# A Mamba block and an FFN on one core: how many gate blocks the first phase leaves to the scan

## The chip, the cores and the metric

The kernel runs on one core of a Trainium2 chip. The core has TensorE (PE in the profile), VectorE (DVE), ScalarE (ACT), GpSimd (POOL) and SyncE (SP), which here issues every DMA. The metric is the device time in microseconds, as the median over several executions. Before the change it is 4656.46 us, from three executions between 4654.45 and 4663.09 us.

## The reference, cut to what matters

Two layers with residuals and layer norms, for 2 sequences of 4096 tokens of width 512:

```
h_in, gate = split(x_norm @ in_proj_w.T)           # 1024 channels each
u  = silu(conv4(h_in) + conv_b)
ts, Bm, Cm = split(u @ x_proj_w.T)                  # 128, 16, 16
dt = softplus(ts @ dt_proj_w.T + dt_proj_b)
h[t] = exp(dt * A) * h[t-1] + dt * u * Bm           # 16 states a channel
y  = (sum_n h * Cm + D * u) * silu(gate)
x  = x + norm(y @ out_proj_w.T)
x  = x + norm(ffn(norm(x)))                         # 512 -> 2048 -> 512, relu,
                                                    # 4-bit weights with LoRA terms
```

What matters here is `silu(gate)`: it is needed only at the end of the scan, so the product `x_norm @ in_proj_w.T` for its 1024 channels can be made at any time before the scan comes to those tokens.

## The kernel before

Tokens are cut into 16 groups of 512 (`NG`, `G`), and a group into four blocks of 128 tokens (`J`). Every product of full precision is three matmuls (`mm3`, L98): both operands are split into a high and a low part in fp32r.

**Phase A** (to L703) goes through the groups, and in each through 8 channel blocks (`block(g, ib)`, L510). A block makes h_in of 128 channels (`h_mm`, 12 matmuls of 512 columns), its convolution (`h_conv`, three DVE instructions), u and its split (`h_rest`), the x_proj sums of an earlier block (`x_proj`), and for the group before it dt (`dt_mm`, softplus) and its transposes (`q_out`). In `ib == 7` the next group's x is transposed into `xnh` and `xnl` (`turn_x`, L163: four PE transposes, an ACT copy, a DVE subtraction); nothing of the next group can start without them. Between all this, FFN weights are dequantised (`prep_ffn`) and stored.

The gate is made in *gate blocks* (`gate_block`, L446): 128 tokens by 512 channels, 12 matmuls of 512 columns, a silu on ACT, a store to `g_d`. A group has 8 of them (four rows of tokens, two halves of channels). Groups 0, 1 and 15 make all 8 in phase A. Groups 2 to 14 make the blocks of rows 0 and 1 there, one each at `ib` 0, 3, 4 and 7 (the tuple on L547), and leave rows 2 and 3 to the scan: for these `turn_x` stores the split x to `xg_d` (L171). 13 groups times 2 rows are 26 blocks for each half of the channels.

**Phase B** (from L706) is the scan. Its unit of order is the *slot*: one DVE scan instruction (`scan`, L950) of 8 states by 64 tokens by 128 channels; there are 2080. For a slot PE makes the input term b (`make_b`, two matmuls of 256 columns), ACT makes exp(dt*A) (`make_exp`, L921), POOL multiplies h by C (L977), and PE sums over states with transposes into PSUM (`nsum`, L997). `slots[e]` is the slot at which group e's last scan is done.

Beside the scan runs a list of other PE work, `tail(g)`, one per stage. A stage begins at slot `start[g]`, ten slots before a group's scans are done: `start` is 0, 134, 262, 390 and so on, 128 or 144 slots apart. Stage 0 holds the gate blocks that were left, first half of the channels (`gates(0)`, L1023). Stage 1 holds the out_proj of the first group (`out_proj`, L1121), then the second half (`gates(1)`). Stages 2 to 15 hold the out_proj of a group and the FFN of the one before.

The pace is a budget in `pe[0]` (L1485): each matmul adds its assumed cost, and after each slot work is taken from the tail until the budget for that slot is used. `GD` (L1083) is a cost without work: a pause before the first gate block of a half. What is left of a tail when its stage ends is emitted at once (L1473). ACT, SP, PE and POOL keep the order in which this program emits, except around the seam between A and B, where the two phases' instructions are interleaved; DVE is ordered by a scheduler.

In `gates`, x of a block is fetched two blocks ahead (`x_in`), its PSUM result is copied to SBUF (L1063), and four results together (`GB`, L1084) get their silu (L1070), so that ACT changes between the tables of exp and silu once per four blocks; then they are stored to `g_d`. SP issues all of it in one queue, with the scan's loads.

Of the kernel before, what the change touches and what calls it, by code (L numbers as in the profile page):

```python
# [8 lines left out]
F32 = mybir.dt.float32  # L9
# [5 lines left out]
P = 128  # L15
# [5 lines left out]
def f32(ap):  # L21
    return ap.bitcast(F32)
# [3 lines left out]
def kernel(  # L26
# [7 lines left out]
    nc = tc.nc  # L34
# [7 lines left out]
    KH, KI, KF = H // P, I // P, HID // P  # L42
# [3 lines left out]
    dram = ctx.enter_context(tc.tile_pool(name="dram", bufs=1, space=DRAM))  # L46
# [9 lines left out]
    NG, J = NT // G, G // P  # L56
# [5 lines left out]
    g_d = [dram.tile([KI, G, P], F32, name=f"g_d{g}") for g in range(NG)]  # L62
    B_d = dram.tile([2, NT, 2, N], F32, name="B_d")
    C_d = dram.tile([NB, NW, N, U], F32, name="C_d")
    GS, JS = 2, 2
    xg_d = [dram.tile([J - JS, P, 2, KH, P], F32, name=f"xg_d{g}") for g in range(NG - 1)]
    wg_d = [dram.tile([P, KH, 512], F32, name=f"wg_d{k}") for k in range(4)]
    y_d = [dram.tile([KI, G, P], F32, name=f"y_d{g}") for g in range(NG)]
    x1_d = [dram.tile([J, P, H], F32, name=f"x1_d{g}") for g in range(NG)]
# [47 lines left out]
    with ExitStack() as sa:  # L117
# [15 lines left out]
        ps_m = sa.enter_context(tc.tile_pool(name="psA", bufs=2, space=PSUM))  # L133
        ps_t = sa.enter_context(tc.tile_pool(name="ptA", bufs=2, space=PSUM))
# [28 lines left out]
        def turn_x(g, xt, j, pool=ps_t):  # L163

            tp = pool.tile([P, KH, P], F32, name=f"tp{g}_{j}", tag="m" if pool is ps_m else "t")
            for kt in range(KH):
                nc.tensor.transpose(tp[:, kt, :], xt[j][:, kt * P:(kt + 1) * P], ident)
            s = slice(j * P, (j + 1) * P)
            nc.scalar.copy(xnh[:, :, s], tp)
            nc.vector.tensor_sub(xnl[:, :, s], tp, f32(xnh[:, :, s]))  # L170
            if j >= JS and GS <= g < NG - 1:  # L171
                for e, t in enumerate((xnh, xnl)):
                    nc.sync.dma_start(xg_d[g][j - JS, :, e], f32(t[:, :, s]))

        def prep_split(w, store, nm, l):

# [319 lines left out]
        GATES = {0: [(j, hf) for hf in range(2) for j in range(J)], 1: [(j, hf) for j in range(J) for hf in range(2)]}  # L496
        GPL = {0: (0, 0, 0, 2, 2, 2, 1, 1), 1: (1,) * 8, NG - 1: (1, 1, 1, 1, 1, 1, 0, 0)}
# [3 lines left out]
        def gate(g, st, fs):  # L501

            if st["gates"]:
                fs.append(gate_block(g, st, *st["gates"].pop(0)))
# [5 lines left out]
        def block(g, ib):  # L510
# [12 lines left out]
            fs = []  # L523

            def evict():
                while fs:
                    fs.pop(0)()
# [9 lines left out]
            def q():  # L537
                if qm:
                    q_out(*qm.pop(0))
# [4 lines left out]

            def gates(late=False):
                if st and late == (2 <= g < NG - 1):
                    for _ in range(GPL.get(g, (1, 0, 0, 1, 1, 0, 0, 1))[ib]):  # L547
                        gate(g, st, fs)


# [1 line left out]
            if ib == 0:  # L552
                q()
            elif ib in (1, 2):
                z(2)
            elif ib == 7 and g + 1 < NG:
                left = {j for j, _ in st["gates"]} if g >= 2 else {J - 1}
                if g < 2:
                    gates()
                    evict()  # L560
                turn = [j for j in range(J) if j not in left] + sorted(left)
                for pool in (ps_m, ps_t):
                    turn_x(g + 1, st["xt"], turn.pop(0), pool)
            if b and ib != 4:
                h_rest((b - 1) // KI, last, (b - 1) % KI)
# [77 lines left out]
            if old:  # L643
                for _ in range(MPL[ib]):
                    i = old["muls"]
# [11 lines left out]

        for g in range(NG):
            groups[g] = {"pm": {}, "u": [], "us": [], "v": [], "muls": 0,
                         "gates": list(GATES.get(g, GATES[1][:2 * JS] if g < NG - 1 else GATES[1]))}  # L660
            if g == 0:
                halo_in(0, 0)
            for ib in range(KI):
                block(g, ib)
            groups.pop(g - 1, None)

        g, old, fs = NG, groups[NG - 1], []
# [6 lines left out]
        x_proj(NG - 1, old, KI - 1)  # L674
        x_out(NG - 1, old)
        gate(NG - 1, old, fs)
        while qm:
            q_out(*qm.pop(0))
        for f in fs:
            f()  # L680
        while dq:
            dq.pop(0)()
        dus.append((NG - 1, old, KI - 1))
# [22 lines left out]
    with ExitStack() as sb:  # L706
# [80 lines left out]
        now, due = [0], {}  # L787

        def at(t, f):
            due.setdefault(max(t, now[0] + 1), []).append(f)  # L790
# [138 lines left out]
        pe = [0.0]  # L929
        TB, TT, TM = 0.125, 0.107, 0.235  # L930
# [92 lines left out]
        def gates(hf, following):  # L1023

            w = [c1.tile([P, KH, 512], FR, name=f"wg{hf}_{e}", tag="xh" if e == 0 else "xl") for e in range(2)]
            for kt in range(KH):
                for e in range(2):
                    nc.sync.dma_start(f32(w[e][:, kt]), wg_d[2 * hf + e][:, kt])
            if hf:
                yield  # L1030

            def x_in(g, j):
                t = wn_.tile([P, 2, KH, P], FR, name=f"xg{hf}_{g}_{j}", tag="wn")
                nc.sync.dma_start(f32(t), xg_d[g][j - JS])
                return t

            todo_ = [(g, j) for g in range(GS, NG - 1) for j in range(JS, J)]
            held = []

            def let_go(f):  # L1040

                while f in held:
                    held.pop(0)()

            raw, nxt = [], [x_in(*q) for q in todo_[:1 + hf]]
            pe[0] += GD[hf]
            yield
            for i, (g, j) in enumerate(todo_):
                t = nxt.pop(0)
                if i == 0 and not hf:  # L1050
                    nxt.append(x_in(*todo_[1]))
                if i >= len(todo_) - 2:
                    following.send(None)
                if len(held) > 1:
                    let_go(held[0])
                pm = (ps_a if hf else ps_w).tile([P, 512], F32, name=f"pz{hf}_{g}_{j}", tag=f"a{i % J}" if hf else "w")
                for kt in range(KH):
                    mm3b(pm, t[:, 0, kt], t[:, 1, kt], w[0][:, kt], w[1][:, kt], kt == 0, kt == KH - 1)
                    yield
                    if kt == 1 and i + 2 < len(todo_):  # L1060
                        nxt.append(x_in(*todo_[i + 2]))
                z = row(f"z{hf}_{g}_{j}")
                held.append(lambda z=z, pm=pm: nc.scalar.copy(z, pm))  # L1063
                at(now[0] + 2, lambda f=held[-1]: let_go(f))
                raw.append((g, j, z))
                if len(raw) == GB or i == len(todo_) - 1:
                    def silu(raw=raw):
                        let_go(held[-1] if held else None)
                        for _, _, z in raw:
                            nc.scalar.activation(z, z, AF.Silu)  # L1070

                    def store(raw=raw):
                        for g_, j_, z in raw:
                            nc.sync.dma_start(g_d[g_][4 * hf:4 * hf + 4, j_ * P:(j_ + 1) * P, :].rearrange("k p i -> p k i"), z.rearrange("p (k i) -> p k i", i=P))

                    at(now[0] + 3, silu)
                    at(now[0] + 5, store)
                    raw = []
            let_go(held[-1] if held else None)
            ahead[hf] = following.send(None)  # L1080
            yield

        GD = 6.5, 10.0  # L1083
        GB = 4  # L1084

        def new_acc(nm):
            return [ps_a.tile([P, H], F32, name=f"{nm}_{j}", tag=f"a{j}") for j in range(J)]
# [323 lines left out]
        C1 = KI * J * (3 * TM + TT)  # L1411
        CF = KF * (KH + J) * 3 * TM + J * KH * TT
# [13 lines left out]
        LEAD = 0  # L1426
        PH = 10
        start = [LEAD] + [slots[e] - PH for e in ends]

        def tick():  # L1430

# [33 lines left out]
        todo, g = iter(()), -1  # L1465
        for k in range(len(units)):
            exp = make_exp(k + 1) if k + 1 < len(units) else iter(())
            n = slots[k + 1] - slots[k]
            for i in range(n):
                slot = slots[k] + i  # L1470
                assert slot == now[0]
                if g < NG and slot >= start[g + 1]:
                    for _ in todo:  # L1473
                        pass
                    g += 1
                    todo, pe[0] = tail(g), 0.0
                    cost = C1 + CF if g > 1 else (C1 if g else 0) + KH * 3 * TM * (NG - 1 - GS) * (J - JS) + GD[g]
                    length = start[g + 1] - start[g] if g < NG else 2 * U
                    cost += length * (2 * TB + (2 * NH + 1) * TT / NU)
                for _ in range(3 if n > 2 else 1):  # L1480
                    next(exp, None)
                scan(k, i // 2, i % 2, slot)
                make_b(slot + 2)
                tick()
                while g >= 0 and pe[0] < cost * (slot + 1 - start[g]) / length and next(todo, 0) is None:  # L1485
                    pass
            for _ in exp:
                pass
# [57 lines left out]
```

## Time and profile before

| | us |
|---|---|
| median of three executions | 4656.46 |
| the profiled execution | 4660.94 |
| its span | 4659.1 |
| phase A, to the first scan | 995.0 |
| first ten slots (scans) | 50.4 |
| rest of stage 0, 124 slots | 180.4 |
| stage 1, 128 slots | 220.3 |
| stage 2, 128 slots | 211.5 |
| stage 3, 128 slots | 210.1 |

The profile comes from one execution. *Busy* is the time in which an engine's instructions ran; matmuls are pipelined and their ends are modelled (a 512-column matmul is shown with 0.39 us where the next starts 0.23 us later), so a gap that PE shows is idle for certain, and small waits are hidden. *PEclk* is the TensorE clock granted, 1.00 being full speed. The DMA share is the mean busy share of the 16 DMA engines and can go a little over 1 in a short window.

### The profile page before, as it was taken

How to read it: one execution, taken by the hardware profiler on the slowest of the kernel's cores; microseconds unless marked ns; L12 is line 12 of the kernel's file. 1: busy time of each engine (PE TensorE's matmuls, PEld its weight loads, DVE VectorE, ACT ScalarE, POOL GpSimd, SP SyncE). 2: the span in 40 equal slices, each digit the busy share in tenths (PEclk: the TensorE clock that was granted, in tenths of full speed). 3: DMA queues.
4: the chain of work that ended last, by engine and by line, in shares of the span. 5: the costliest groups of instructions: out<-in, count | busy, mean ns of one | idle time of the engine just before them, and what ended most of it. 6: DMA issues, size and time to landing. Idle time of an engine off the chain costs nothing.

```text
span 4659.1 us, 85017 instructions
## 1 busy us (share of the span) xinstructions
PE 4485.4 (96%) x26613; PEld 3872.2 (83%) x26613; DVE 3845.0 (83%) x6273; ACT 3308.1 (71%) x7324; POOL 3274.7 (70%) x2360
## 2 busy tenths in 40 slices
PE   8999999968899999999999989999999999999999
PEld 6777777757788888888888878888888888888887
DVE  6677777749888999999999989899999999999931
ACT  5777777768688676767677767777686767767643
POOL 1333333339797888889898889888898988888820
PEclk9999999979999999999999999999999999999999
DMA  4888888768889888879788877788797878888765
GB/s 146 260 253 256 258 257 257 231 188 227 244 223 258 228 240 222 251 219 261 220 247 226 239 200 227 229 231 253 211 261 219 253 215 247 226 240 237 218 233 195
DMA packets 1139315, 1083.93 MB, mean 233 GB/s; under 512 B 142583, under 2 KB 912399, under 8 KB 1138872
## 3 DMA queue, kind: packets, MB, share of 16 engines
q1 hardware_dynamic: 1138872, 1078.50, 80.2%
q8 instruction: 220, 3.60, 0.3%
q14 instruction: 223, 1.83, 0.1%
HBM read 800.87 MB, written 277.29 MB: 231 GB/s over the span
## 4 chain that ended last, share of the span: by engine, by line
PE 73%; DMA 7%; DVE 6%; POOL 5%; ACT 4%; issue 3%; SPq 2%; DVEq 0%; POOLq 0%; ACTq 0%
PE yp L997 15%; PE b L947 8%; PE pu L99 5%; PE pu L100 5%; PE pu L101 5%; PE fa L99 4%; PE fa L100 4%; PE fa L101 4%; DVE h L965 3%; POOL pr L977 3%; PE pm L100 2%; PE pm L99 2%; PE pm L101 2%; POOL bd L807 2%; PE pg L99 1%
## 5 line engine op out<-in xcount | busy, mean ns | idle before, releaser
L977 POOL TENSOR_TENSOR pr<-h,cb 128x1008 f32<-128x1008 f32 (+1 forms) x1056 | 2453.3, 2336 | 474.2 <-DVE b L964 276.7
L965 DVE TENSOR_TENSOR_SCAN h<-dA,b 128x512 f32<-128x512 f32 x2080 | 2535.4, 1220 | 142.0 <-PE b L947 13.7
L921 ACT ACTIVATE dA<-dt,A 128x252 f32<-128x252 f32 x4096 | 1702.4, 496 | 161.1 <-DVE h L965 145.5
L997 PE MATMUL yp<-ident,pr 128*126 128x128 f32 (+1 forms) x8448 | 1104.7, 274 | 19.1 <-DVE xl L1260 7.4
L997 PEld LDWEIGHTS yp<-ident,pr 128*126 128x126 f32 (+1 forms) x8448 | 951.4, 140 | 28.3 <-POOL pr L977 10.5
L947 PEld LDWEIGHTS b<-bd,d 128*128 128x128 f32 x4160 | 752.1, 189 | 215.3 <-POOL bd L807 21.6
L947 PE MATMUL b<-bd,d 128*128 128x256 f32 x4160 | 875.2, 291 | 54.5 <-DMA d<-dT_d 17.9
L1307 ACT ACTIVATE pu<-pu,bu 128x512 f32<-128x512 f32 x256 | 168.7, 659 | 602.5 <-PE pu L101 602.5
L437 DVE SCALAR_TENSOR_TENSOR pm<-hin,cw,pm 128x512 f32<-128x512 f32 x384 | 288.0, 750 | 210.9 <-ACT pm L434 203.8
L99 PE MATMUL fa<-wn,hh 128*128 128x512 f32 x1024 | 421.2, 411 | 0.0
L99 PE MATMUL pu<-xh,wu 128*128 128x512 f32 x960 | 402.3, 419 | 7.6 <-DMA wu<-wu_d 7.4
L100 PE MATMUL fa<-wn,hh 128*128 128x512 f32 x1024 | 403.6, 394 | 0.0
L101 PE MATMUL fa<-wn,hl 128*128 128x512 f32 x1024 | 401.0, 392 | 0.0
L100 PE MATMUL pu<-xl,wu 128*128 128x512 f32 x960 | 378.2, 394 | 0.0
L101 PE MATMUL pu<-xh,wu 128*128 128x512 f32 x960 | 375.9, 392 | 0.0
L433 POOL COPY halo<-hin 128x3 f32<-128x3 f32 x128 | 28.0, 219 | 460.5 <-ACT hin L432 460.5
L964 DVE COPY b<-h 128x8 f32<-128x8 f32 x1536 | 254.1, 165 | 106.2 <-PE b L947 99.6
L1311 DVE TENSOR_TENSOR hl<-pu,hh 128x512 fp32r<-128x512 f32 x256 | 172.0, 672 | 152.0 <-ACT hh L1309 152.0
L807 POOL TENSOR_TENSOR bd<-dl,bp 128x512 fp32r<-128x512 f32 x260 | 271.7, 1055 | 14.7 <-PE z L101 14.7
L101 PEld LDWEIGHTS fa<-wn,hl 128*128 128x128 f32 x1024 | 192.3, 188 | 44.9 <-DVE hl L1311 0.6
L101 PEld LDWEIGHTS pu<-xh,wu 128*128 128x128 f32 x960 | 180.3, 188 | 42.0
L99 PE MATMUL pm<-xnh,Wih 128*128 128x512 f32 x512 | 207.0, 404 | 4.4 <-ACT u L442 2.9
(584 smaller groups left out, 7787.6 us busy)
## 6 DMA issues: line engine op xcount, KB each, us to landing
d<-dT_d SPq DMA_DIRECT2D x1040, 128.0 KB
wu<-wu_d SPq DMA_DIRECT2D x256, 512.0 KB
wn<-wn_d SPq DMA_DIRECT2D x256, 512.0 KB
cb<-C_d SPq DMA_DIRECT2D x128, 512.0 KB
wo<-wo_d SPq DMA_DIRECT2D x128, 512.0 KB
dd_d<-du SPq DMA_DIRECT2D x128, 256.0 KB
dd_d<-v SPq DMA_DIRECT2D x128, 256.0 KB
ys<-y_d SPq DMA_DIRECT2D x128, 256.0 KB
```

What stands on the lines that cost most here:

```text
L99: nc.tensor.matmul(ps, ah, bh, start=start, stop=False)
L100: nc.tensor.matmul(ps, ah, bl, start=False, stop=False)
L101: return nc.tensor.matmul(ps, al, bh, start=False, stop=stop)
L437: cv = nc.vector.scalar_tensor_tensor(pm, hin[:, k:k + G], cw[:, ib, k:k + 1], pm, ALU.mult, ALU.add)
L807: nc.gpsimd.tensor_mul(tb, dl.unsqueeze(1).to_broadcast([P, N, 32]), bp[:, w // 2, w % 2, :].unsqueeze(2).to_broadcast([P, N, 32]))
L921: nc.scalar.activation(dA[2 * (k % 2) + hf][:, :n_, m, 1:U], dtv, AF.Exp, scale=A[:, ib, n:n + 1])
L947: nc.tensor.matmul(b[:, :, v * 32:(v + 1) * 32], t4[:, u if l is None else l, v, :], Bd[2 * u + v][:, hf * NH:(hf + 1) * NH, :], start=Tru ...
L964: nc.vector.tensor_copy(b[:, :, 0], hs["prev"][:, hf])
L965: scans.append(nc.vector.tensor_tensor_scan(h[:, uu].rearrange("p n t -> p (n t)"), dAt[:, u].rearrange("p n t -> p (n t)"), b.rearrange(" ...
L977: nc.gpsimd.tensor_mul(to, h[:, :uu + 1, :, f:], Cb[j, hf][:, :uu + 1, :, f:])
L997: nc.tensor.matmul(yp[:m], pr[:, n, :m], ident, is_transpose=True, start=(hf == 0 and n == 0), stop=False)
L1311: nc.vector.tensor_sub(hl, pu, f32(hh))
```

## The change

- `JS`, the first row of a group that is left to the scan, becomes a list: 4 (none left) for groups 0, 1 and 15, 2 for groups 2 and 3, 1 for groups 4 to 14. Eleven groups leave three rows of four. Phase A makes 22 gate blocks less; each half in the scan has 37 and not 26.
- These eleven groups make their two remaining blocks at `ib` 3 and 4; those at `ib` 0 and 7 are gone.
- In `ib == 7` the first two transposed blocks of x use the PSUM pool `ps_t` both, not `ps_m` and `ps_t`.
- At the end of phase A the last two gate blocks get their silu before the last two `q_out`, not after.
- `GD` has three entries: stage 0 pauses 5.5 before the first x is fetched and 3.0 after it (6.5 after it before); stage 1 pauses 10.0 as before.
- `GB` is 4 for the first half and 2 for the second. Silu and store come one slot earlier after the last matmul.
- `start[1] += 4`: stage 1, with the out_proj of the first group, begins four slots on, and stage 0 is four slots longer.

```diff
-    GS, JS = 2, 2
+    GS = 2
+    JS = [J] * GS + [2] * 2 + [1] * (NG - GS - 3) + [J]
...
-            if j >= JS and GS <= g < NG - 1:
+            if j >= JS[g]:
...
-                    for _ in range(GPL.get(g, (1, 0, 0, 1, 1, 0, 0, 1))[ib]):
+                    for _ in range(GPL.get(g, (1, 0, 0, 1, 1, 0, 0, 1) if JS[g] == 2 else (0, 0, 0, 1, 1, 0, 0, 0))[ib]):
...
-                for pool in (ps_m, ps_t):
+                for pool in (ps_t, ps_t):
...
-                         "gates": list(GATES.get(g, GATES[1][:2 * JS] if g < NG - 1 else GATES[1]))}
+                         "gates": list(GATES.get(g, GATES[1][:2 * JS[g]]))}
...
         gate(NG - 1, old, fs)
+        for f in fs:
+            f()
         while qm:
             q_out(*qm.pop(0))
-        for f in fs:
-            f()
...
-            todo_ = [(g, j) for g in range(GS, NG - 1) for j in range(JS, J)]
+            todo_ = [(g, j) for g in range(NG) for j in range(JS[g], J)]
...
+            if not hf:
+                pe[0] += GD[0]
+                yield
             raw, nxt = [], [x_in(*q) for q in todo_[:1 + hf]]
-            pe[0] += GD[hf]
+            pe[0] += GD[1 + hf]
...
-                if len(raw) == GB or i == len(todo_) - 1:
+                if len(raw) == GB[hf] or i == len(todo_) - 1:
...
-                    at(now[0] + 3, silu)
-                    at(now[0] + 5, store)
+                    at(now[0] + 2, silu)
+                    at(now[0] + 4, store)
...
-        GD = 6.5, 10.0
-        GB = 4
+        GD = 5.5, 3.0, 10.0
+        GB = 4, 2
...
+        start[1] += 4
...
-                    cost = C1 + CF if g > 1 else (C1 if g else 0) + KH * 3 * TM * (NG - 1 - GS) * (J - JS) + GD[g]
+                    cost = C1 + CF if g > 1 else (C1 if g else 0) + KH * 3 * TM * sum(J - j for j in JS) + (GD[2] if g else GD[0] + GD[1])
```

More of the change, by code (lines that the diff above doesn't have):

```diff
@@ L64 @@
     C_d = dram.tile([NB, NW, N, U], F32, name="C_d")
-    GS, JS = 2, 2
-    xg_d = [dram.tile([J - JS, P, 2, KH, P], F32, name=f"xg_d{g}") for g in range(NG - 1)]
+    GS = 2
+    JS = [J] * GS + [2] * 2 + [1] * (NG - GS - 3) + [J]
+    xg_d = [dram.tile([J, P, 2, KH, P], F32, name=f"xg_d{g}") for g in range(NG - 1)]
     wg_d = [dram.tile([P, KH, 512], F32, name=f"wg_d{k}") for k in range(4)]
@@ L170, in turn_x @@
             nc.vector.tensor_sub(xnl[:, :, s], tp, f32(xnh[:, :, s]))
-            if j >= JS and GS <= g < NG - 1:
+            if j >= JS[g]:
                 for e, t in enumerate((xnh, xnl)):
-                    nc.sync.dma_start(xg_d[g][j - JS, :, e], f32(t[:, :, s]))
+                    nc.sync.dma_start(xg_d[g][j, :, e], f32(t[:, :, s]))
         def prep_split(w, store, nm, l):
@@ L1033, in x_in @@
                 t = wn_.tile([P, 2, KH, P], FR, name=f"xg{hf}_{g}_{j}", tag="wn")
-                nc.sync.dma_start(f32(t), xg_d[g][j - JS])
+                nc.sync.dma_start(f32(t), xg_d[g][j])
                 return t
-            todo_ = [(g, j) for g in range(GS, NG - 1) for j in range(JS, J)]
+            todo_ = [(g, j) for g in range(NG) for j in range(JS[g], J)]
             held = []
```

## The prediction

> **What bounds the kernel now.** I read the page's first parts, then busy time by stage, then the chain of instructions at one group boundary of phase A and at the seam, and last the waits of PE in the first two stages of the scan. By stage (start and end, length, then busy us and count of PE, PEld, DVE, ACT, POOL, then granted clock, DMA share, GB/s):
>
> ```profile
> 0.00:975.00 975.00, 924.99 (x4265) 721.59 (x4266) 687.49 (x1120) 699.16 (x1189) 302.43 (x483) 0.99 0.78 237
> 975.00:995.00 20.00, 13.04 (x47) 8.62 (x46) 3.94 (x8) 13.51 (x32) 2.38 (x6) 0.72 0.71 186
> 995.00:1045.40 50.40, 23.30 (x117) 18.75 (x116) 27.42 (x31) 27.30 (x66) 20.20 (x19) 0.57 0.66 197
> 1045.40:1225.80 180.40, 164.84 (x1092) 145.88 (x1091) 166.92 (x277) 141.67 (x321) 164.88 (x103) 0.99 0.80 224
> 1225.80:1446.10 220.30, 202.62 (x1258) 178.95 (x1257) 181.31 (x297) 169.06 (x371) 176.10 (x107) 0.97 0.85 240
> 1657.60:1867.70 210.10, 208.02 (x1334) 185.60 (x1333) 192.66 (x316) 152.96 (x363) 182.16 (x114) 1.00 0.86 236
> ```
>
> The last row is stage 3, which stands for all that follow: PE is busy 99%, and sets 1.64 us a slot. Stages 0 and 1 and the seam have PE to spare. The change moves PE work there from phase A, where PE is busy 95%; the total of PE work stays. So the time changes by what PE's idle time changes, and the question is whether A really shrinks by the work taken out and whether the scan has room.
>
> At a group boundary of A the DVE has no gap for 6.7 us (start, length, instruction, idle before it):
>
> ```profile
> 552.87 0.69 DVE L384 TENSOR_TENSOR qs_3l<-qt,qs_3h 128x512 fp32r<-128x512 f32 x1 [0.27 <-DMA dT_d<-qs_0l]
> 553.47 0.68 DVE L259 TENSOR_TENSOR pw_0s<-pw_0p,pw_0s 128x512 f32<-128x512 f32 x1
> ...
> 557.59 0.74 DVE L437 SCALAR_TENSOR_TENSOR pm<-hin,cw,pm 128x512 f32<-128x512 f32 x1
> 558.32 1.29 DVE L170 TENSOR_TENSOR xnl<-tp,xnh 128x512 fp32r<-128x512 f32 x2
> ...
> 566.01 0.68 DVE L95 TENSOR_TENSOR us_7l<-u,us_7h 128x512 fp32r<-128x512 f32 x1
> ```
>
> and PE at the same place:
>
> ```profile
> 559.78 0.39 PE L100 MATMUL pm<-xnl,Wih 128*128 128x512 f32 x1
> ...
> 564.26 0.48 PE L99 MATMUL pg<-Wih,xnh 128*128 128x512 f32 x1
> ...
> 567.46 0.48 PE L99 MATMUL ts<-us_7h,Wxh 128*128 128x512 f32 x1
> ```
>
> The reader is to see that the next group's first low matmul (559.78) starts 0.17 us after the last xnl is there (558.32 + 1.29), and that x_proj of the last block (567.46) comes 0.8 us after its us_7l (566.69).
>
> **The change part by part.** The sum is made against the profiled execution, 4660.94 us (span 4659.1 and 1.8 around it), 4.5 above the median of 4656.46.
>
> *A gate block in phase A.* Matmuls of 512 columns start 0.23 us apart, so 12 are 2.76 us, and 22 are 60.7 us. What comes off the path is less. At `ib` 7 the block stood between the second and the third transpose. In the changed kernel's program DVE has the same ten instructions in that stretch, in nearly the same order, and no gate work. So the last xnl still comes 6.7 us after qs_3l starts: 559.55 where it was 559.61. The gain is 0.05 us at most boundaries. At two (near 317 and 434) the gate block ran at a reduced clock and ended late; there it is 1.5 us. At `ib` 0 the block stood ahead of x_proj 7, which now waits for us_7l: 0.95 us here, 1.2 by the same rows of the other groups. Sum: 11 x 1.2 + 3 = 16 us. Against it stands the idle time that is left: PE has 1.7 us between the second and third transpose, since `ps_t` has two buffers and the third must wait for the first xnl. Gaps of this size were followed by a reduced clock:
>
> ```profile
> 320.19 0.50 PE L99 MATMUL pg<-Wih,xnh 128*128 128x512 f32 x1 [1.79 <-DVE pw_0s L259]
> ```
>
> ```profile
> 320.00:324.50 4.50, 4.32 (x13) 3.35 (x14) 4.29 (x8) 0.57 (x1) 1.28 (x1) 0.67 1.00 310
> ```
>
> The clock was 0.67 over these 4.5 us, 1.5 us lost. If two boundaries in three get this and most of it is covered by the DVE chain, some 0.5 us each, 5 us in all. I take -11 us; ends -61 (all of the blocks on the path) and +8 (1.7 us lost at each of eleven boundaries is 19 against the 16 gained, and 0.35 us at each of fifteen for the first transposes, which in `ps_t` wait on qs_2l and qs_3l, is 5).
>
> [...]
>
> *Stores and loads in A.* A left row is stored as two DMAs of 256 KB to `xg_d`; two gate stores of 256 KB go. Bytes and issues on SP are equal: 0, ends -1 and +3 (the xg stores wait on SP for their xnl, with the loads for the next weights behind them).
>
> *The seam.* Silu of the last gate blocks ahead of the q copies frees the PSUM that the first z waits for (idle 1.23 us). More weighs that in the changed program all eight v and softplus stand before the first exps; before, exps stood between them, and ACT loaded tables five times at 1.28 us from 980.98 to 1007.34 where two are left. Then everything waited for a load behind the last 4 MB of stores:
>
> ```profile
> 1021.28 0.69 DVE L384 TENSOR_TENSOR qs_7l<-qt,qs_7h 128x512 fp32r<-128x512 f32 x1 [0.91 <-ACT qs_7h L379]
> 1034.99 1.28 DVE L909 TENSOR_TENSOR dA<-dt,A 128x504 f32<-128x504 f32 x2 [13.01 <-DMA dt<-dd_d]
> ```
>
> From the same rows: eight v at 0.69 from 980 end at 985.5; one load and eight softplus at 0.54 at 991 (1007.3 before); one load and four units of exps at 2.5 at 1002.5; two q copies among them 1003.6; six more at 1.25 end at 1011 (1021.3 before). The DMA has the same bytes and starts them earlier. I take 14 us earlier; ends -17 (all of the 16 us by which softplus is earlier, and the 1.23) and +4 (the wg loads now stand behind the v stores on SP, and the first gate block with them).
>
> *Stages 0 and 1.* Stage 3 gives a slot's price at full packing: it holds 484 matmuls of 512 columns (384 FFN, 96 out_proj, 4 bias) and 48 transposes at 0.11; (210.1 - 111.3 - 5.3) / 128 = 0.73 us a slot for the scan itself. The stretch from slot 10 to slot 262 then has 252 x 0.73 + (624 + 96) x 0.23 + 32 x 0.11 = 353 us of work and takes 400.7: 47.6 us over full packing. With 22 blocks more it is 413.8, if nothing stalls: +13. If every one of the 47.6 us stays it is +61. Those that stay are the ones in which PE, which keeps its order, waits for something that is not the scan: in stage 1
>
> ```profile
> L1107 PE MATMUL ty<-ident,ys 128*128 128x128 f32 x32 | 5.0, 279 | 8.9 <-DMA ys<-y_d 7.8 <-issue 1.1
> ```
>
> the four slots of delay give the y stores 6 us more, so I let 4 of the 8.9 stay; 3.5 on xg loads in stage 0; 2.5 on a result's copy; the reduced clock after such gaps (0.97 over 220 us is 6.6); and the time in which ACT does silu and not exps, where slots 80 to 100 ran at 1.6 us against 1.4 (4 us). That is 21. I take +34.
>
> ACT in stage 1 is the part that grows most: 11 copies and silus at 0.57 and 0.54 are 12 us, and two blocks a silu give some 37 table loads for 15, 22 x 1.28 = 28 us: 169 becomes 209 us of about 230. The DMA gets 11 x (512 + 256) KB = 8.4 MB on 52.8 MB: its share goes from 0.85 to 0.95. Both still fit. What SP queues behind the 22 more x loads and 22 more stores are the scan's dt, d and cb loads; they are issued units ahead, and what covers them is gone if the DMA is full.
>
> *The rest.* Pauses, silu one slot earlier, the larger `xg_d`: 0, hidden by a PE that is the bound; ends -3 and +3. From stage 2 on nothing changes.
>
> Sum: -11 - 14 + 34 = +9 us. On the median: 4666.
>
> **Rivals.**
> (1) *The scan packs fully.* If with more work at hand PE never waits outside the scan, stages 0 and 1 cost 13 and not 34: -11 - 14 + 13 = -12, 4645, faster. For it: the largest wait, on ys, gets 6 us more time. Against: 8.9 us of ys wait came with a DMA share of 1.06, and the DMA gets fuller. It decides from where the two stages grow by less than 25 us.
> (2) *Phase A gives the whole work back*, -61: with half of the scan's stalls gone, -61 - 14 + 34 = -41, 4616. Against: the DVE rows above.
> (3) *ACT and DMA bound stage 1.* If 209 us of ACT and a DMA at 0.95 don't overlap with the order PE wants, and stage 1 takes 20 us more: +29, 4686; for it: ACT has 91% to do, and every burst of silu stops the exps for 3.6 us.
> (4) *The change doesn't do what it says*: the blocks are in the program's order as described; none.
>
> **How the numbers follow.** Forecast 0.42, (1) 0.23, (2) 0.07, (3) 0.23, anything else 0.05. What can be told from no change is 0.2%, 9.3 us. The forecast's own range, 4652 to 4680 (its terms by 14 either way), lies half above that bound, hardly below it; (1) lies two thirds below; (2) below; (3) above. Faster 0.27, same 0.23, slower 0.50. For 8 in 10 the range runs from half of the way between (1) and (2) to past (3): 4632 to 4700.
>
> **What would show it.** Right: first scan near 984, ten slots on by about 1020; PE gaps of some 1.7 us at the boundaries from group 4 to 14, and groups only 1 to 2 us shorter; stages 0 and 1 PE busy over 95%, each longer by 10 to 25 us. Wrong: groups shorter by 4 us or more; stage 1 no longer than before; an ACT with idle time in stage 1 and PE at 99%.

## The result

The changed kernel takes 4693.92 us (median of four executions, 4685.22 to 4698.46), the kernel before beside it 4657.02: 1.0079 times as long, 95% interval 1.0066 to 1.0092. The profiled executions, 4689.76 and 4660.94 us, are 28.8 apart, and divide so:

| part | before | after | predicted | measured |
|---|---|---|---|---|
| phase A, to the first scan | 995.0 | 983.7 | -11 | -11.3 |
| seam, first ten slots | 50.4 | 43.7 | -14 | -6.7 |
| slots 10 to 262 (stages 0 and 1) | 400.7 | 449.5 | +34 | +48.8 |
| slot 262 to the end | 3213.0 | 3211.1 | 0 | -1.9 |

Busy time by stage after the change (start and end, length, then busy us and count of PE, PEld, DVE, ACT, POOL, then granted clock, DMA share, GB/s); the cuts are 965, the first scan, slot 10, slot 138 (where stage 1 now begins), slot 262, and stage 3:

```profile
0.00:965.00 965.00, 882.56 (x4004) 679.21 (x4005) 685.99 (x1121) 691.87 (x1168) 301.50 (x483) 0.98 0.79 240
965.00:983.70 18.70, 12.17 (x54) 8.55 (x53) 7.39 (x11) 15.97 (x28) 5.65 (x8) 0.84 0.80 223
983.70:1027.40 43.70, 20.26 (x101) 15.95 (x101) 21.79 (x27) 20.15 (x66) 17.47 (x18) 0.60 0.77 218
1027.40:1229.40 202.00, 194.10 (x1248) 172.42 (x1247) 177.33 (x288) 164.18 (x355) 170.90 (x107) 0.99 0.89 243
1229.40:1476.90 247.50, 229.16 (x1368) 199.34 (x1367) 181.36 (x288) 206.86 (x409) 171.33 (x103) 0.98 0.88 250
1690.10:1900.40 210.30, 208.14 (x1334) 185.73 (x1333) 193.02 (x318) 152.96 (x363) 182.39 (x114) 1.00 0.84 236
```

PE was busy 94.9% of phase A (up to its last 20 us) and is now busy 91.5%: the work has gone and most of its time has stayed. The boundary of group 9, DVE first (start, length, instruction, idle before it):

```profile
548.38 0.69 DVE L385 TENSOR_TENSOR qs_3l<-qt,qs_3h 128x512 fp32r<-128x512 f32 x1 [1.71 <-DMA dT_d<-qs_0l]
548.99 0.68 DVE L260 TENSOR_TENSOR pw_0s<-pw_0p,pw_0s 128x512 f32<-128x512 f32 x1
...
553.02 0.76 DVE L438 SCALAR_TENSOR_TENSOR pm<-hin,cw,pm 128x512 f32<-128x512 f32 x1
553.68 1.29 DVE L171 TENSOR_TENSOR xnl<-tp,xnh 128x512 fp32r<-128x512 f32 x2
```

and PE there:

```profile
549.12 0.66 PE L168 MATMUL tp<-ident,xt 128*128 128x128 f32 x4 [1.75 <-DVE qs_3l L385]
551.31 1.97 PE L168 MATMUL tp<-ident,xt 128*128 128x128 f32 x8 [1.53 <-DVE xnl L171]
...
555.55 0.39 PE L101 MATMUL pm<-xnl,Wih 128*128 128x512 f32 x1
...
561.81 0.47 PE L100 MATMUL ts<-us_7h,Wxh 128*128 128x512 f32 x1
```

From qs_3l to the last xnl DVE takes 6.6 us, where it took 6.7; the first low matmul (555.55) comes 0.58 us after it. Where the gate block stood, between the second transpose (549.12) and the last two (551.31), PE now waits 1.53 us. Ahead of the second transpose it waits 1.75 us (0.20 before), for a qs_3l that itself waited 1.71 us for a store to dT_d, to which `q_out` sends its rows. The clock follows (windows of the same view as above; a stretch with a granted clock of one half is called a half-clock stretch from here on):

```profile
547.60:551.00 3.40, 0.66 (x4) 0.42 (x4) 2.62 (x5) 1.57 (x3) 1.07 (x2) 1.00 0.86 249
551.00:554.40 3.40, 3.09 (x12) 2.69 (x13) 3.40 (x7) 1.79 (x3) 1.01 (x1) 0.51 1.02 318
554.40:557.80 3.40, 3.40 (x18) 2.79 (x17) 1.26 (x2) 1.21 (x2) 0.00 (x0) 0.99 1.02 287
```

At the seam, the last q split and the first instruction behind the late load (DVE):

```profile
1005.47 0.69 DVE L385 TENSOR_TENSOR qs_7l<-qt,qs_7h 128x512 fp32r<-128x512 f32 x1 [1.51 <-DMA dT_d<-qs_3h]
1015.24 1.28 DVE L910 TENSOR_TENSOR dA<-dt,A 128x504 f32<-128x504 f32 x2 [9.07 <-DMA dt<-dd_d]
```

The split is 15.8 us earlier, 4.5 more than phase A gave, and the wait for dt fell from 13.0 to 9.1.

In stage 1 the added time lies in its later part. Its first 90 us and the rest, before and after:

```profile
1225.80:1316.00 90.20, 76.08 (x467) 66.74 (x466) 70.45 (x116) 58.87 (x135) 65.30 (x41) 0.94 0.80 227
1316.00:1446.10 130.10, 126.54 (x793) 112.21 (x792) 110.86 (x182) 110.19 (x236) 110.80 (x67) 0.99 0.89 249
```

```profile
1229.40:1320.00 90.60, 79.39 (x465) 68.51 (x464) 64.79 (x103) 57.85 (x131) 58.23 (x36) 0.94 0.86 238
1320.00:1476.90 156.90, 149.76 (x905) 130.83 (x904) 116.57 (x185) 149.00 (x279) 113.10 (x68) 1.00 0.89 257
```

Before, 14.1 of the 17.7 us in which PE shows idle were in the first 90 us, with the out_proj and the pause; of the 332 gate matmuls recorded in the stage (26 blocks are 312; the others are left from stage 0), PE has 39 there and 293 behind them. The later part was 97% busy. After the change it holds 392 of them, one slot more, and is 26.8 us longer; the 99 more are 22.8 us at 0.23, so they found no idle time there.

### The profile page after: what moved, and what is told of

The parts are those of the page before. It is cut to its first block, busy times and chain, and to the rows that moved or that the text cites. A ratio compares the mean times of both kernels' runs of the same rounds, so it can differ in the third digit from the quotient of the medians.

```text
span 4688.0 us, 85135 instructions
## 1 busy us (share of the span) xinstructions
PE 4496.1 (96%) x26613; PEld 3875.4 (83%) x26613; DVE 3853.2 (82%) x6273; ACT 3357.1 (72%) x7371; POOL 3274.3 (70%) x2360
## 4 chain that ended last, share of the span: by engine, by line
PE 70%; DMA 8%; POOL 6%; DVE 6%; ACT 5%; issue 4%; SPq 1%; POOLq 0%; DVEq 0%; ACTq 0%
PE yp L998 14%; PE b L948 8%; PE pu L100 4%; PE pu L101 4%; PE pu L102 4%; PE fa L100 4%; PE fa L101 4%; PE fa L102 4%; POOL pr L978 3%; DVE h L966 2%; PE pm L101 2%; PE pm L100 2%; PE pm L102 2%; PE ca L100 2%; PE ca L101 2%
## 5 line engine op out<-in xcount | busy, mean ns | idle before, releaser
L101 PEld LDWEIGHTS fa<-wn,hh 128*128 128x128 f32 x1024 | 193.8, 189 | 20.2
```

Of the source, the lines that this page charges most:

```text
L101: nc.tensor.matmul(ps, ah, bl, start=False, stop=False)
```

## The experiments

The theory: gate blocks in phase A fill waits of PE and give nothing back; in the scan, stage 0 has idle PE for some of them, stage 1 none where they stand. The rivals: ACT's table loads, or the DMA, bound stage 1; or the other edits make the loss. Twelve runs were made, two of them of the two kernels as they are. The kernel before had medians of 4644.5, 4654.3, 4649.7 and 4652.6 us beside them, so ratios are compared, each to the kernel before in its own series.

### e1_rest: all edits but the moved blocks

```diff
-    JS = [J] * GS + [2] * 2 + [1] * (NG - GS - 3) + [J]
+    JS = [J] * GS + [2] * (NG - GS - 1) + [J]
```

> The changed kernel with the old number of blocks: groups 2 to 14 all leave two rows of four (26 blocks for each half), all the other edits stay (the two transposes in ps_t, silu ahead of the last q copies, the split pause, two results a silu in the second half, stage 1 four slots later). Theory (the blocks that moved are the whole loss; the rest is worth the seam): first scan within 4 us of 995 or earlier, ten slots on by 1038 (7 us less than 1045.4), stages 0 and 1 together within 5 us of their 400.7, the time 4645 to 4655. Rival (two results a silu: table loads on ACT are what makes stage 1 long): stage 1 longer by 10 us or more with the old number of blocks too, the time 4660 or more.

4643.11 us, ratio 0.9997 (0.9988 to 1.0007). First scan 985.3, ten slots on 1026.4, slots 10 to 262 404.2 us. The theory holds: the other edits together make no loss, and the loss comes with the blocks. But phase A is 9.7 us shorter than in the first profile of the kernel before, with all its blocks in place. (The whole profile is 18.7 us shorter, where the ratio of the medians shows 0.03%: a single profile tells less than its digits.) Groups 4 to 14 here, and then in the changed kernel:

```profile
259.60:891.90 632.30, 616.94 (x2892) 479.10 (x2892) 476.56 (x767) 483.44 (x815) 213.37 (x331) 1.00 0.86 260
```

```profile
259.00:890.00 631.00, 580.02 (x2640) 441.97 (x2640) 476.83 (x767) 472.31 (x794) 211.55 (x331) 0.98 0.87 261
```

The moved blocks make 252 matmuls less in the trace and 37 us less of busy PE (58 at 0.23 each; some that are left show longer, as the last two transposes of group 9, 1.97 us where they took 1.03); the eleven groups are 1.3 us shorter. Two results a silu don't lengthen stage 1 by themselves: 217.6 us in 124 slots, where it was 220.3 in 128, or 217.4 without four slots at 0.73.

### b_again, a_again: both kernels again

> The kernel before, unchanged, for a profile from the same chip as the other runs. Theory (the two transposes in one pool make phase A about 10 us shorter, the blocks that left it nothing): first scan at 993 to 997, as in the first profile, and the groups of phase A 57 to 60 us each. Rival (the 10 us are a difference between chips): first scan at 984 to 987.

One execution, 4666.9 us: first scan 994.4, groups of 57 to 60 us. Phase A of 994 to 995 us is not a matter of the first chip.

> The changed kernel, unchanged, on the same chip. Expected: 1.0079 times the kernel before, within 0.002; stage 1 (slots 138 to 262) 245 to 251 us. With two results a silu it should stand 3 to 8 us under the run with four, if that run's longer stage 1 (255.1) is not chance; the rival is that both take the same.

4695.53 us, ratio 1.0085 (1.0069 to 1.0101), stage 1 248.1 us, first scan 988.6, which is 4.9 later than in its first profile. The result repeats; a single phase A tells no more than some 5 us.

### e9_pst: the transposes' pool alone

```diff
-                for pool in (ps_m, ps_t):
+                for pool in (ps_t, ps_t):
```

> The kernel before with one edit: the first two transposed blocks of x both in ps_t. Theory (this edit is what shortened phase A): first scan 7 to 10 us before that of the kernel before, no half-clock stretches at the boundaries after the third group, the rest as before: the time 6 to 11 us lower. Rival (the prediction's price: a transpose that waits on the q rows, 0.35 us at each of fifteen boundaries): first scan up to 5 us later, the time the same or up to 5 us higher.

4655.76 us, ratio 1.0002 (0.9991 to 1.0012), first scan 991.7. Neither: 2.7 to 3.3 us earlier than in the two profiles of the kernel before, and the half-clock stretches of groups 5 and 7 are still there. In this profile the pool explains a third of the 9.7 us. Up to 960 us the traces of this run, e1_rest and e10_start12 hold the same instructions in the same order on PE, DVE, ACT and POOL, and the first scan came at 991.7, 985.3 and 990.2, with 20.5, 6.8 and 17.1 us of half clock up to 965 us. So a good part of e1_rest's 9.7 us is a difference between executions.

### e4_gates07: the other two blocks moved

```diff
-... if JS[g] == 2 else (0, 0, 0, 1, 1, 0, 0, 0))[ib]):
+... if JS[g] == 2 else (1, 0, 0, 0, 0, 0, 0, 1))[ib]):
```

> The changed kernel, but the eleven groups keep their two blocks at ib 0 and 7 and lose those at ib 3 and 4: as many blocks move, other ones. Theory (the boundary is set by DVE, and the blocks at ib 0 and 7 filled a PE that waits there; at ib 3 and 4 PE is the bound): phase A ends 30 to 50 us earlier than the changed kernel's 983.7, the half-clock stretches at the boundaries are gone, the scan's stages as in the changed kernel, the time 4644 to 4664. Rival (phase A is bound all through by a chain that has no PE work of the gates in it): phase A ends within 5 us of 983.7, the time 4690 to 4700.

4700.89 us, ratio 1.0126 (1.0110 to 1.0141), first scan 996.6: 8 to 13 us later than in the changed kernel. Both expectations fell. PE's waits in groups 4 to 14 (us in total, times, longest):

```profile
PE pm L100 <- ACT u L443: 35.2, 22, 2.5
```

and what ACT does at `ib` 3 there:

```profile
470.32 1.28 ACT L391 ACT_TABLE_LOAD   x1
471.62 4.28 ACT L396 ACTIVATE v<-v 128x512 f32<-128x512 f32 x8
475.91 1.28 ACT L391 ACT_TABLE_LOAD   x1
```

For 6.9 us ACT makes softplus between two table loads, and the silu that frees a pm for the next h_in waits behind it. The blocks at `ib` 3 and 4 fill this wait of PE, as those at `ib` 0 and 7 fill that on DVE.

### e11_warm: six idle matmuls in the gap

```diff
             else:
+                if st and JS[g] == 1:
+                    dm = ps_m.tile([P, 512], F32, name=f"dm{g}", tag="m")
+                    for _ in range(6):
+                        nc.tensor.matmul(dm, Wi[0][0][:, :P], Wi[0][0][:, :512], start=True, stop=True)
                 gates(True)
```

> The changed kernel, and in the eleven groups six more matmuls of 512 columns at ib 7, into a PSUM tile that nothing reads, where a gate block of twelve stood before the change: 66 matmuls in all, 15 us at 0.23. Theory (the reduced clock after the boundary's gaps takes back what phase A would gain): half-clock stretches in phase A fall from eight or nine to three or fewer, the groups from 4 on take 56 to 56.7 us where they took 57.4, phase A ends at 970 to 979, the time 6 to 14 us under the changed kernel's 4695. Rival (DVE's chain sets the boundary whatever the clock): phase A ends within 4 us of 986, the clock restored or not, the time within 5 us of 4695.

4690.91 us, ratio 1.0091 (1.0077 to 1.0105), first scan 980.6; half-clock stretches after 300 us fell from eight to three. The gap of 1.53 us ahead of the last two transposes is gone here (PE, group 9):

```profile
547.13 0.66 PE L168 MATMUL tp<-ident,xt 128*128 128x128 f32 x4 [0.42 <-DVE qs_3l L385]
547.54 1.63 PE L631 MATMUL dm<-Wih 128*128 128x512 f32 x6
549.32 1.09 PE L168 MATMUL tp<-ident,xt 128*128 128x128 f32 x8
```

Between the two theories: groups 4 to 14 took 625.8 us, where the changed kernel's two profiles have 631.0 and 633.2, and phase A ends 5 us before the mean (986.0) of the five profiles with the changed kernel's phase A; the time doesn't show it. By this one profile the reduced clock is some 5 us of phase A, not the 61 that are missing.

### e12_prep5: one dequantisation out of DVE's chain

```diff
-        LPL = (1, 0, 1, 0, 0, 1, 0, 0)
+        LPL = (1, 0, 1, 0, 1, 0, 0, 0)
...
             elif ib == 5:
                 evict()
                 xp()
                 q()
+                prep()
                 q()
             elif ib == 6:
                 xp()
                 q()
-                prep()
                 q()
```

> The changed kernel, with the third FFN block of a group's dequantisation at ib 5 and not 6 (its load one step earlier too): DVE then has no pw instruction among the ten at the boundary, 1.1 us less (0.69 and 0.42) in the stretch from qs_3l to the last xnl. Theory (DVE's chain sets the boundary, so what phase A would gain is got by shortening that chain and not by taking gate blocks from PE): the groups from 4 on are 0.6 to 1.1 us shorter, phase A ends at 972 to 980 where it ended at 984 to 989, the time 6 to 14 us under the changed kernel's 4695. Rival (the chain only shifts: the three instructions make ib 5 and 6 as much later, or the conv and the us subtraction set the boundary): phase A ends within 4 us of 986.

4693.83 us, ratio 1.0090 (1.0074 to 1.0107), first scan 990.3: as the rival has it. But the edit did less than was meant. The two pw instructions left the stretch and a convolution instruction came into it (DVE, group 9):

```profile
551.31 0.68 DVE L385 TENSOR_TENSOR qs_3l<-qt,qs_3h 128x512 fp32r<-128x512 f32 x1
556.34 1.28 DVE L171 TENSOR_TENSOR xnl<-tp,xnh 128x512 fp32r<-128x512 f32 x2
```

From qs_3l to the last xnl DVE takes 6.3 us and not 6.6: 0.3 less and not 1.1, some 3 us over eleven groups, which one profile can't tell. The run doesn't decide.

### e2_gb44, e5_nosilu, e6_nox: ACT and DMA in stage 1

```diff
-        GB = 4, 2
+        GB = 4, 4
```

> The changed kernel with four results a silu in the second half (GB 4, 4). Some 18 table loads of 1.28 us fewer in stage 1, 20 to 23 us less of ACT there (206.9 now). Theory (PE's order and its own work set stage 1): slots 138 to 262 stay within 3 us of 247.5, the time within 4 us of the changed kernel's 4693.9. Rival (ACT, at 0.99 for most of the stage, is the bound): stage 1 shorter by 12 to 20 us, the time 4674 to 4682.

```diff
-                        for _, _, z in raw:
+                        for _, _, z in () if hf else raw:
                             nc.scalar.activation(z, z, AF.Silu)
```

> The changed kernel without the silu of the second half's left blocks: the raw products are stored as they are. Leaves out 37 silus of 0.54 us and the 36 table loads of 1.28 us in stage 1, some 65 us less of ACT there (206.9 now, 142 left of 247). Theory (PE's order and work set stage 1): slots 138 to 262 stay within 4 us of 247.5. Rival (ACT is the bound): they fall to 218 to 228, near the 218 us that the work takes at full packing, and the time to 4665 to 4675.

```diff
+            once = []
+
             def x_in(g, j):
+                if hf and len(once) > 2:
+                    once.append(once[-3])
+                    return once[-1]
                 t = wn_.tile([P, 2, KH, P], FR, name=f"xg{hf}_{g}_{j}", tag="wn")
                 nc.sync.dma_start(f32(t), xg_d[g][j])
+                once.append(t)
                 return t
```

> The changed kernel, but the second half loads x for its first three left blocks only and uses these again; leaves out 34 loads of 512 KB (17.4 MB of 62 MB in stage 1), so its gates are of the wrong rows. Theory (PE's order and work): the 7.0 us of waits for xg go, slots 138 to 262 take 238 to 243 us, the time 4 to 9 us under the changed kernel. Rival (DMA is the bound of stage 1): they take 220 to 230 us, the time 18 to 27 us under.

Slots 138 to 262, four results a silu:

```profile
1230.80:1485.90 255.10, 231.22 (x1368) 201.31 (x1367) 181.56 (x288) 183.18 (x390) 171.61 (x104) 0.96 0.82 242
```

no silu:

```profile
1230.40:1471.40 241.00, 226.83 (x1368) 198.97 (x1367) 181.50 (x288) 145.92 (x342) 171.34 (x104) 0.98 0.87 258
```

no x loads:

```profile
1234.20:1476.40 242.20, 226.14 (x1368) 197.65 (x1367) 181.04 (x288) 205.47 (x406) 171.22 (x103) 0.99 0.65 181
```

The times are 4694.30, 4676.04 and 4691.85 us, the ratios 1.0109 (1.0094 to 1.0124), 1.0069 (1.0049 to 1.0089) and 1.0075 (1.0052 to 1.0098). With 24 us less of ACT the first is 7.6 us longer than the changed kernel's 247.5, where its rival wanted 12 to 20 less and the theory no change: PE's waits for xg went from 7.0 to 11.2 us, the longest from 2.4 to 7.7 (one profile). Without silu, with ACT busy 61%, the stage loses 6.5 us, 2.5 more than the theory allowed and a third of what the rival wanted; with the DMA at 0.65 it loses 5.3 (from 247.5), as the theory had it, and the time is 3.7 under the changed kernel's in its series. The time without silu, 4676.04, comes near the 4665 to 4675 of ACT's rival only because the kernel before was faster in that series (4644.5): the ratios 1.0079 and 1.0085 put the changed kernel at 4681 to 4684 there. So neither ACT nor the DMA by itself bounds stage 1. In both runs PE's waits for xg (7.0 us) are gone, so the two gains of some 6 us seem to be the same wait; they don't add up, and no run took both away.

### e8_half0: the third row left in the first half only

```diff
+    JH = JS, [J] * GS + [2] * (NG - GS - 1) + [J]
...
-... (0, 0, 0, 1, 1, 0, 0, 0))[ib]):
+... (0, 0, 0, 1, 1, 0, 0, 1))[ib]):
...
-                         "gates": list(GATES.get(g, GATES[1][:2 * JS[g]]))}
+                         "gates": [q for q in GATES.get(g, GATES[1]) if q[0] < JH[q[1]][g]]}
...
-            todo_ = [(g, j) for g in range(NG) for j in range(JS[g], J)]
+            todo_ = [(g, j) for g in range(NG) for j in range(JH[hf][g], J)]
```

(and the same list in the stage's cost)

> The changed kernel, but the eleven groups leave the third row in the first half of the channels only: phase A makes three blocks of each (ib 3, 4 and 7), stage 0 has 37 blocks and stage 1 has 26. Theory (stage 0 has idle PE that its blocks can use, stage 1 has none where its blocks stand, and phase A gives next to nothing): slots 0 to 138 take 242 to 248 us, slots 138 to 262 215 to 221, phase A ends at 976 to 988, the ratio to the kernel before 1.001 to 1.005. Rival (a block costs its 2.76 us in either stage): slots 0 to 138 take 254 or more, the ratio is 1.005 to 1.009. Second rival (phase A gives back the block at ib 0): phase A ends at 966 or earlier and the ratio is under 1.

4674.54 us, ratio 1.0060 (1.0044 to 1.0075): slots 0 to 138 250.6 us, slots 138 to 262 217.3, first scan 996.4. Against e1_rest (227.7 and 217.6) the eleven blocks cost stage 0 22.9 us; in the changed kernel's two profiles they cost it 18.0 and 21.7, and the other eleven cost stage 1 29.9 and 30.5, of 30.4 by price. So the two stages differ as the theory has it, though stage 0 absorbs less than it said: its 250.6 lies between the theory's 242 to 248 and the rival's 254, and the ratio lies in the rival's range. Phase A became 8 us longer than expected, with eleven blocks less; why wasn't tried.

### e10_start12: the out_proj of group 0 later

```diff
-        start[1] += 4
+        start[1] += 12
```

on e1_rest's kernel.

> The first run's kernel (all the other edits, old number of blocks), with stage 1 begun twelve slots on and not four. Theory (the idle PE of stage 1 is the out_proj of group 0 waiting for y that was summed just before): the waits for ys in slots 134 to 262 fall from 8.3 us to under 2, slots 0 to 262 take 435 to 440 us where they took 445, the ratio to the kernel before 0.997 to 0.999. Rival (what the out_proj does not wait for, a later block does): slots 0 to 262 within 3 us of 445, the ratio 0.999 to 1.001.

4647.11 us, ratio 0.9993 (0.9984 to 1.0002); slots 0 to 262 449.4 us where e1_rest took 445.3. Nearest the rival, whose 3 us it passes by 1: the ys waits fell from 8.3 to 6.0 us only, and waits for xg (3.5) and pr (3.6) stand beside them. The idle PE at the head of stage 1 is not got back by starting later. No version that ran beats the kernel before.

## Why the prediction was right and wrong

**The whole.** 4666 was forecast. The 4693.92 lie outside the forecast's own range (4652 to 4680), and inside the wide one (4632 to 4700) only near its upper end, which was put there for rival (3). The likelier direction came; two of the three terms were off, and the third agrees by luck.

**Phase A: the size came out, the reason only in part.** -11 was forecast and -11.3 measured. As forecast, DVE kept its stretch (6.6 us), a gap opened where the gate block stood (1.53 us, forecast 1.7), and the reduced clock followed at eight of the eleven boundaries, at about the 5 us that it was given (e11_warm). But the step "11 x 1.2 + 3 = 16 us" of gain is not supported: with the old blocks and the new pool phase A ended at 985.3, 990.2 and 991.7 (e1_rest, e10_start12, e9_pst), mean 989.1; with the changed kernel's blocks it ended at 983.7 to 988.6 in five profiles, mean 986.0. That is 3 us between the means, of 60.7 us of work, and less than the spread of either. The two profiles of the kernel before have 995.0 and 994.4, so most of the -11.3 stands between them and the runs with the new pool and between executions; e9_pst's ratio, 1.0002, shows no gain from the pool. That -11.3 meets -11 is luck. Rival (2), -61, is out: phase A is not bound by PE, although PE was busy 95% of it. That DVE's chain is what binds it is not shown either: e12_prep5 took only 0.3 us out of the chain. What sets the 57 us of a group stays open. One wait grew: in groups 4 to 14 DVE and ACT sit idle 25 us (31 in the second profile) until a store to dT_d has landed, 10 in e1_rest. The DMA, at a share of 0.86 with the blocks and 0.87 without, is a candidate that wasn't tried.

**The clock.** The prediction priced the clock by a row in which a gap of 1.79 us was followed by a clock of 0.67 over 4.5 us, and the row was right: 3.4 us that lay mostly in two gaps of 1.75 and 1.53 us, with PE busy 0.66 us, were followed by 3.4 us at 0.51. In the changed kernel's first profile the half-clock stretches up to 965 us last 3.41 or 6.83 us, and they start and end on one grid of 3.413 us: two of them start at 435.00 and 551.05, 34 times 3.413 apart. Cut along this grid from 100 to 965 us, this profile has 9 pieces at full clock that were followed by one at half clock, and PE shows busy in 1 to 52% of each; 232 were not, and PE shows busy in 55% or more of each. A piece at half clock was followed by full clock with PE busy 87% or more (9 pieces), by another at half clock with 65% or less (3). In the five profiles with the changed phase A together the four are 43 (0 to 53%), 1155 (52% or more), 43 (81% or more) and 22 (79% or less). So here the clock went to half after 3.41 us in which PE shows busy about half or less, and two gaps of under 1.8 us were enough for that.

**The seam: mis-sized.** -14 was forecast, -6.7 measured. The direction and the cause hold: every profile with the edits at the seam has 41.1 to 44.1 us here, the three without 49.7 to 50.4; and ACT loads tables (1.28 us each) twice there in the changed kernel and in e1_rest, five times in the kernel before and in e9_pst. The term that failed is the q splits, which were to end 10 us earlier of themselves and ended 4.5 earlier: the last three wait 1.5 to 1.6 us each for an earlier store to dT_d. So slot 10 came at 1027.4 and not at 1020.

**Stages 0 and 1: the step that failed.** Of 47.6 us over full packing the prediction let 21 stay, and 35.7 stay (449.5 - 413.8). It treated the idle time of both stages as one pool that any gate block can use. Stage 0 used 11.7 us of its own (it grew by 21.6, where 11 blocks and four slots at 0.73 are 33.3), and 7.0 in the second profile. Stage 1 used 0.3 (it grew by 27.2, where 11 blocks less four slots are 27.5), and nothing in the second: its idle PE stands ahead of most gate blocks in PE's order (before the change, 14.1 of 17.7 us with 39 of 332 gate matmuls), and where the blocks stand it was 97% busy. The prices are shown by e8_half0; that the place of the idle time is the reason is read from the trace, as no run put blocks into it. Two of the prediction's signs of being right fell with this: stage 1 has PE busy 93% and not over 95%, and is 27 us longer and not 10 to 25.

**Rival (3) has the nearer time, 4686, but not the mechanism.** ACT came out at 206.9 us as priced (209), the DMA share at 0.88 and not 0.95. Taking ACT's silu or the x loads away gave 5 to 7 us each, not the 20 that (3) put on them. Rival (1), that the scan packs fully, is out with 48.8 measured where it had 13.

## What to carry to other kernels

An engine that is busy 95% need not be the bound: its work may be filling waits that would be there without it, and moving it out then earns little (here some 3 of 61 us). Before moving work into a stage's slack, find where in the engine's order the slack lies; idle time ahead of the new work is of no use to it. One profile of a phase with seven or eight half-clock stretches is good to some 5 us here, so a single part's agreement with a forecast is no proof of its reason.

## What was not expected of the hardware

The same phase A, instruction for instruction, ended between 983.7 and 988.6 us in five profiles, with seven or eight half-clock stretches after 300 us at changing boundaries. It went with where a gap falls on the grid of 3.41 us: in the changed kernel's first profile the gap of 1.53 us at 606.80 lies in one piece of the grid, with PE busy 1.72 us, and half clock followed; that at 721.35 lies in two, with PE busy 2.24 us in each, and none followed. And in one profile a longer silu burst, with 24 us less of ACT work in the stage, went with a stage 7.6 us longer, with one wait of 7.7 us for a load of x in it.
